# A fixed order of TensorE's work in a two-layer graph attention kernel: fillers between producers and consumers, masks one chunk per beat, two projection chunks per PSUM bank, a second weight queue

## The chip, the core and the metric

The kernel runs on one core of one Trainium2 chip. The metric is the device time of one execution in microseconds (us), lower is better. Each kernel is timed several times in rounds that alternate with the kernel before on the same chip.

The engines: TensorE (PE in the profile; PEld is its weight load), VectorE (DVE), ScalarE (ACT), GpSimd (POOL) and SyncE (SP, which issues transfers). SBUF is the working memory, PSUM the accumulators that TensorE writes.

## The reference, cut to what matters

There are 32 graphs of 512 nodes with 256 features. Each passes through two layers. The first is a transformer layer with masked attention and an MLP, with an outer residual and norm; the second is masked attention with a residual and a norm.

```python
# layer 0
allowed = (adj > 0) | (swapaxes(adj, 1, 2) > 0) | eye          # mask 0
scores  = where(allowed, (q * scale) @ k.T, -inf)              # 8 heads of 32
x1 = layernorm(x + softmax(scores) @ v @ Wo.T + bo) * g1 + be1
h  = layernorm(x1 + relu(x1 @ W1.T + b1) @ W2.T + b2) * g2 + be2
x  = layernorm(x + h)
# layer 1
mask = adjacency == 0                                          # mask 1
x  = layernorm(x + softmax(where(mask, -inf, scores)) @ v @ Wo.T + bo)
```

## The kernel before

The program is a list of 64 slots. A slot is the attention of one graph in one layer, in eight "beats": scores of a chunk of 128 keys for four heads (TensorE), the exponential (ScalarE), the multiply with the 0/1 mask (VectorE), and the product with the values (TensorE). Between the beats, the slot carries other graphs' work. A "forward" slot carries the MLP of the graph whose layer 0 has just ended. An "output" slot carries the output of the graph whose layer 1 has just ended, and the masks of a new graph. The order of emission below is the order on each engine. The comments are mine.

```python
ps_d = pools.enter_context(tc.tile_pool(name="ps_d", bufs=2, space=PSUM))  # two banks for all that is not attention

def masked(self, layer, k):                      # VectorE: the mask multiply, 128 x 2048
    p, m = self.p[k], (self.m0, self.m1)[layer]
    nc.vector.tensor_tensor(p, p, m[:, k % NQ, None, :].to_broadcast([P, HPC, N]), ALU.mult)

def mask0(self, i):                              # TensorE builds adj | adj.T | eye in PSUM ...
    ps = ps_d.tile([P, N], F32, tag="d", name=f"psM_{self.b}_{i}")
    ...
    nc.vector.tensor_scalar(self.m0[:, i, :], ps, 0.0, None, ALU.is_gt)       # ... VectorE empties the bank

def mask1(self, i):
    ps = ps_d.tile([P, N], F32, tag="d", name=f"psN_{self.b}_{i}")
    ...
    nc.vector.tensor_scalar(self.m1[:, i, :], ps, 0.0, None, ALU.not_equal)

def residual(self):                              # GpSimd: two row additions over 128 x 1024
    add_row(self.tile("x1", [NQ, D]), self.x, bov[0])
    add_row(self.x, self.x, be2)

def out1(self, i):                               # one chunk of the projection per bank
    ps = self.projected(1, i)
    y = small.tile([P, D], F32, tag="y", name=f"yl_{self.b}_{i}")
    nc.vector.tensor_tensor(y, ps, self.x2[:, i, :], ALU.add)
    self.y[i] = y, self.statistics(y, 4, i)      # two on VectorE, then add and power on GpSimd

for k in range(BEATS):                           # the output slot, cut
    g.scores(layer, k)
    if k > 0:
        g.masked(layer, k - 1)
    ...
    if k == 2:
        for i in range(NQ):
            last.out1(i)
            if i > 0:
                last.norm4(i - 1)
    elif k == 3:
        last.norm4(NQ - 1); last.store()
        for h in range(2): new.transpose(new.x, h)
        new.residual(); new.mask0(0)
    elif k == 4: new.mask0(1); new.mask0(2)
    elif k == 5: new.mask0(3); new.mask1(0); new.mask1(1)
    elif k == 6: new.mask1(2); new.mask1(3)
    elif k == 7: new.value(0, 0)
    g.product(layer, k - 2)
```

All weights come in on SyncE's queue, ahead of the first graph's x.

## Time and profile before

| | before |
|---|---|
| time, median of the first 3 runs | 3988.58 us (3986.46 to 3989.38) |
| first scores | 45.1 us |
| first slot | 41.3 us |
| forward slot (32 of them) | 72.27 or 73.95 us |
| output slot (30), mean | 50.35 us |
| last slot with the tail | 52.8 us |

A slot is read from the timeline of TensorE as the time from its first scores to the first scores of the next slot.

### The profile page before, as it was taken

The page shows a single profiled execution, that of the slowest core. Times are in us where ns is not written, and L with a number is a line of the kernel's source. Part 1 is how long each engine was busy: PE and PEld are TensorE (multiplying, and loading weights), DVE is VectorE, ACT ScalarE, POOL GpSimd, SP SyncE. Part 2 cuts the span into 40 slices and gives each one's busy share as a digit, 9 for nine tenths or more (in the row PEclk, how much of TensorE's full clock was granted, in tenths as well). Part 3 has the DMA queues.
Part 4 walks back from the last instruction along what each step waited for, and adds up shares of the span by engine and source line. Part 5 has one row for each costly group of instructions (what it writes and reads, how often), then busy time and mean ns, then how long its engine had stood idle before and what let it go on. Part 6 is the DMA issues. An engine that isn't in the chain of part 4 may idle for free.

```text
span 3988.9 us, 51603 instructions
## 1 busy us (share of the span) xinstructions
PE 3643.6 (91%) x21514; PEld 1862.8 (47%) x21514; DVE 2523.0 (63%) x3461; ACT 1606.8 (40%) x1729; POOL 1147.4 (29%) x1545
## 2 busy tenths in 40 slices
PE   7999989899998998989999899998999989999898
PEld 3544535444353443534435354453544535445354
DVE  4566575766757567575665756657566675665765
ACT  3434444334443344344343443434444344343443
POOL 1332322323223132332323323232231322313222
PEclk9999999999999999999999999999999999999999
DMA  2000000000000000000000000000000000000000
GB/s 83 17 22 12 26 11 17 22 22 17 11 17 27 17 22 6 17 27 17 22 6 17 27 17 22 6 17 27 17 22 6 29 15 17 22 6 32 11 1 12
DMA packets 57553, 75.61 MB, mean 19 GB/s; under 512 B 4448, under 2 KB 40416, under 8 KB 57312
## 3 DMA queue, kind: packets, MB, share of 16 engines
q1 hardware_dynamic: 57312, 72.24, 5.5%
q8 instruction: 170, 2.79, 0.3%
q14 instruction: 71, 0.58, 0.0%
HBM read 55.45 MB, written 16.78 MB: 18 GB/s over the span
## 4 chain that ended last, share of the span: by engine, by line
PE 67%; DVE 26%; ACT 3%; POOL 2%; issue 2%; DVEq 0%; ACTq 0%; POOLq 0%
DVE p L277 12%; PE psH L363 12%; PE psF L381 11%; PE psA L290 10%; PE psR L298 9%; PE psQK L255 7%; PE psS L268 7%; PE psV L240 6%; DVE cT L316 3%; PE psO L345 2%; DVE x L406 2%; POOL rs L326 2%; DVE m L209 2%; PE psT L228 2%; ACT xT L231 1%
## 5 line engine op out<-in xcount | busy, mean ns | idle before, releaser
L272 ACT ACTIVATE p<-psS 128x2048 f32<-128x2048 f32 x512 | 961.9, 1879 | 1382.8 <-PE psS L268 1382.8
L277 DVE TENSOR_TENSOR p<-p,m 128x2048 f32<-128x2048 f32 x512 | 1217.4, 2393 | 111.3 <-ACT p L272 111.3
L309 DVE STREAM_TRANSPOSE sT<-psR 128x512 f32<-128x512 f32 x128 | 91.8, 717 | 1074.6 <-PE psR L298 1074.6
L268 PE MATMUL psS<-qT,kT 32*128 32x512 f32 x4096 | 590.5, 646 | 51.8 <-ACT kT L258 51.0
L290 PE MATMUL psA<-p,v 128*32 128x512 f32 x4096 | 555.2, 614 | 1.0 <-DVE p L277 1.0
L298 PE MATMUL psR<-p,ones 128*32 128x512 f32 x4096 | 551.5, 611 | 0.0
L363 PE MATMUL psH<-xT,w_L_gnn_W 128*128 128x256 f32 x2048 | 467.7, 384 | 23.4 <-ACT xT L231 23.4
L326 POOL TENSOR_TENSOR rs<-rs,neg_half 128x1 f32<-128x1 f32 x512 | 462.8, 904 | 42.7
L312 POOL TENSOR_TENSOR total<-total,sT 128x16 f32<-128x16 f32 x128 | 29.0, 226 | 1546.7 <-DVE sT L309 1546.7
L381 PE MATMUL psF<-w_L_gnn_W,hT 128*128 128x256 f32 x2048 | 459.1, 382 | 0.0
L363 PEld LDWEIGHTS psH<-xT,w_L_gnn_W 128*128 128x128 f32 x2048 | 381.2, 190 | 130.0 <-ACT xT L231 55.2
L325 POOL TENSOR_SCALAR rs<-mv 128x1 f32<-128x1 f32 x512 | 213.9, 418 | 789.0 <-DVE mv L324 781.7
L381 PEld LDWEIGHTS psF<-w_L_gnn_W,hT 128*128 128x128 f32 x2048 | 383.8, 190 | 100.7 <-ACT cT L306 26.8
L268 PEld LDWEIGHTS psS<-qT,kT 32*128 32x128 f32 x4096 | 162.8, 186 | 438.0 <-issue 206.7
L371 ACT ACTIVATE hT<-psH,c_L_gnn_b 128x256 f32<-128x256 f32 x512 | 215.0, 471 | 269.0 <-PE psH L363 267.5
L345 PE MATMUL psO<-w_L_gnn_Wo,cT 128*128 128x256 f32 x1024 | 254.2, 395 | 45.2 <-DVE y L339 22.4
L298 PEld LDWEIGHTS psR<-p,ones 128*32 128x32 f32 x4096 | 135.7, 112 | 314.7 <-issue 309.0
L345 PEld LDWEIGHTS psO<-w_L_gnn_Wo,cT 128*128 128x128 f32 x1024 | 179.3, 189 | 142.7 <-ACT kT L258 47.8
L255 PE MATMUL psQK<-xT,w_L_gnn_Wqkv 128*128 128x512 f32 x512 | 236.7, 605 | 0.0
L164 POOL TENSOR_TENSOR x<-x,s_L_gnn_b 128x1024 f32<-128x1024 f32 x32 | 75.4, 2356 | 386.8 <-PE psT L228 386.8
L290 PEld LDWEIGHTS psA<-p,v 128*32 128x32 f32 x4096 | 83.9, 108 | 195.7 <-issue 174.0
L231 ACT COPY xT<-psT 128x512 f32<-128x512 f32 x192 | 109.3, 588 | 122.5 <-PE psT L228 122.5
(68 smaller groups left out, 3363.5 us busy)
## 6 DMA issues: line engine op xcount, KB each, us to landing
adj<-in_adj_dram SPq DMA_DIRECT2D x32, 1024.0 KB, 6.2
x<-in_x_dram SPq DMA_DIRECT2D x32, 512.0 KB, 3.9
out_dram<-x SPq DMA_DIRECT2D x32, 512.0 KB, 2.9
w_L_gnn_W<-in_L_gnn_W_dram SPq DMA_DIRECT2D x2, 1024.0 KB, 9.8
w_L_gnn_Wqkv<-in_L_gnn_Wqkv_dram SPq DMA_DIRECT2D x1, 768.0 KB, 4.8
w_L_gnn_Wo<-in_L_gnn_Wo_dram SPq DMA_DIRECT2D x2, 256.0 KB, 4.4
s_L_gnn_bo<-in_L_gnn_bo_dram SPq DMA_DIRECT2D x2, 128.0 KB, 5.3
s_L_gnn_ln_g<-in_L_gnn_ln_g_dram SPq DMA_DIRECT2D x2, 128.0 KB, 5.6
```

The costliest lines, as they stand in the source:

```text
L240: nc.tensor.matmul(ps[:, j, :], self.xT[:, i, at], proj[layer][0][2][:, i, :], start=(i == 0), stop=(i == ND - 1),)
L255: nc.tensor.matmul(ps, w[:, i, c * P : (c + 1) * P], self.xT[:, i, :], start=(i == 0), stop=(i == ND - 1))
L268: nc.tensor.matmul(s[:, j, :], self.kT[at, hg, kc * P : (kc + 1) * P], self.qT[at, hg, :], start=True, stop=True)
L272: nc.scalar.activation(p, s, AF.Exp, scale=SCALE)
L277: nc.vector.tensor_tensor(p, p, m[:, k % NQ, None, :].to_broadcast([P, HPC, N]), ALU.mult)
L290: nc.tensor.matmul(a[j * HD : (j + 1) * HD, :], self.v[:, kc, h * HD : (h + 1) * HD], p[:, j, :], start=(kc == 0), stop=(kc == NQ - 1),)
L298: nc.tensor.matmul(s[j * HD : (j + 1) * HD, :], ones, p[:, j, :], start=(kc == 0), stop=(kc == NQ - 1))
L326: nc.gpsimd.tensor_tensor(rs, rs, neg_half[:, 0:1], ALU.pow)
L345: nc.tensor.matmul(ps, self.cT[:, k, i * P : (i + 1) * P], wo[layer][:, k, :], start=(k == 0), stop=(k == ND - 1))
L363: nc.tensor.matmul(ps[:, j, :], w1[:, c, at], self.xT[:, c, h * 2 * P : (h + 1) * 2 * P], start=(c == 0), stop=(c == ND - 1),)
L371: nc.scalar.activation(self.hT[h][:, f + j, :], ps[:, j, :], AF.Relu, bias=b1[:, f + j : f + j + 1])
L381: nc.tensor.matmul(ps, self.hT[h][:, f, j * P : (j + 1) * P], w2[:, f, :], start=(f == 0), stop=(f == NF - 1))
```

## The change

The intent is that TensorE never comes to a consumer directly after the producer that it has to wait for. The loop with its conditions becomes two straight lists (`slot_forward`, `slot_output`) with other work between each producer and its consumer. A chunk's two masks are built together, one chunk per beat. Two chunks of the output projection share a PSUM bank. All weights but the first layer's q, k and v move to ScalarE's queue.

```diff
+    def queue(name):
+        return nc.sync if "qkv" in name else nc.scalar
...
+            def project(self, layer, h):
+                ps = ps_d.tile([P, 2, D], F32, tag="d", name=f"psO_{self.b}_{layer}_{h}")
+                for j in range(2):
+                    at = slice((2 * h + j) * P, (2 * h + j + 1) * P)
...
             def out1(self, i):
-                ps = self.projected(1, i)
...
+                self.residual_statistics(self.po[i // 2][:, i % 2, :], self.x2, 4, i)
...
+        def slot_forward(g, layer, last, later):
...
+            g.scores(layer, 7)
+            last.norm2(3)
+            g.masked(layer, 6)
+            last.norm3(2)
+            last.norm3(3)
+            g.masked(layer, 7)
+            g.product(layer, 5)
+            last.transpose(last.x2, 0)
+            g.product(layer, 6)
+            last.value(1, 0)
+            last.transpose(last.x2, 1)
+            g.product(layer, 7)
+            last.query_key(1, 0, 0)
+            last.query_key(1, 1, 0)
+            last.value(1, 1)
...
+        def slot_output(g, layer, last, new, later):
...
+                last.project(1, 0)
+                last.project(1, 1)
+                last.out1(0)
+                last.out1(1)
...
+                new.transpose(new.x, 1)
+                new.residual()
+            g.product(layer, 1)
             for i in range(NQ):
...
+                attend(g, layer, 4 + i)
+                if new:
+                    new.mask0(i)
+                    new.mask1(i)
+                g.product(layer, 2 + i)
```

## The prediction

> **What bounds the kernel now.** I read the page first, then TensorE's waits, then TensorE in order of time over two graphs (1023 to 1272 us), then VectorE and GpSimd there.
>
> ```profile
> PE 3643.6 (91%) x21514; PEld 1862.8 (47%) x21514; DVE 2523.0 (63%) x3461; ACT 1606.8 (40%) x1729; POOL 1147.4 (29%) x1545
> ```
>
> TensorE is busy 91% of a span of 3988.9 us, so its idle time is 345 us. Its waits (who waited for what: us in total, times, longest) say where that is:
>
> ```profile
> PE psN L215 <- DVE m L209: 69.4, 32, 2.3
> PE psS L268 <- ACT kT L258: 51.0, 64, 1.1
> PE psM L203 <- ACT xT L231: 45.0, 31, 1.5
> PE psV L240 <- DVE m L218: 30.2, 29, 1.6
> PE psH L363 <- ACT xT L231: 23.4, 32, 0.7
> PE psV L240 <- ACT xT L231: 23.4, 32, 0.7
> PE psO L345 <- DVE y L339: 22.4, 16, 1.4
> PE psO L345 <- DVE yl L401: 22.4, 16, 1.4
> PE psB L158 <- DMA w_L_gnn_Wo<-in_L_gnn_Wo_dram: 21.6, 2, 14.0
> PE psQK L255 <- ACT xT L231: 21.6, 32, 0.7
> ```
>
> Each but psB is a producer directly ahead of its consumer, or a PSUM buffer not yet emptied; they add to 309 us. The busy time hides one more loss. Columns below: stretch, length, busy us of PE, PEld, DVE, ACT, POOL, TensorE's granted clock, DMA share, GB/s:
>
> ```profile
> 1006.00:1007.00 1.00, 1.00 (x12) 0.13 (x4) 0.11 (x1) 0.59 (x1) 0.00 (x0) 0.70 0.08 16
> 1007.00:1008.00 1.00, 1.00 (x9) 0.21 (x8) 0.09 (x1) 0.00 (x0) 0.00 (x0) 0.50 0.00 0
> 1008.00:1009.00 1.00, 1.00 (x8) 0.31 (x8) 0.93 (x3) 0.00 (x0) 0.23 (x1) 0.50 0.00 0
> ```
>
> After the 2.29 us wait of psN (to 1004.96) the clock is halved from 1006.4 to about 1009.8, which makes 1.7 us of work last 3.4. The same follows the next psN wait at 1053.85. At 32 such waits that is an estimated 54 us more.
>
> The program has 64 slots, each the attention of one graph in one layer. 32 "forward" slots also carry another graph's MLP; 32 "output" slots carry another graph's output and a new graph's masks. Scores to scores, a forward slot takes 72.27 us (1073.28 to 1145.55) or 73.95 (to 1219.50), and output slots average 50.35: between 86.36 and 3936.06 there are 15 times four slots and two forward ones, so (3849.7 - 146.2) / 15 = 246.9 for four. Start (45.1) + first slot (41.3) + 16 x 146.2 + 30 x 50.35 + last slot and tail (52.8) = 3989, the span.
>
> The third view decides how much can be won. VectorE and GpSimd in the output slot (start, length, engine, line):
>
> ```profile
> 1040.18 2.29 DVE L277 TENSOR_TENSOR p<-p,m 128x2048 f32<-128x2048 f32 x1
> 1042.92 2.45 DVE L406 TENSOR_SCALAR x<-yl,mv,rs 128x256 f32<-128x256 f32 x1 [0.45 <-POOL rs L326]
> 1045.29 0.68 DVE L209 TENSOR_SCALAR m<-psM 128x512 bf16<-128x512 f32 x1
> 1045.89 3.90 DVE L277 TENSOR_TENSOR p<-p,m 128x2048 f32<-128x2048 f32 x1
> ```
> ```profile
> 1040.42 2.46 POOL L326 TENSOR_TENSOR rs<-rs,neg_half 128x1 f32<-128x1 f32 x1
> 1042.86 2.36 POOL L164 TENSOR_TENSOR x<-x,bov 128x1024 f32<-128x1024 f32 x1
> 1045.29 2.35 POOL L164 TENSOR_TENSOR x<-x,s_L_gnn_ln_b 128x1024 f32<-128x1024 f32 x1
> ```
>
> A mask multiply (L277) held GpSimd's tiny power up to 2.46 us (0.57 alone); then GpSimd's two row additions held a normalization 2.45 us (0.38 alone) and a multiply 3.90 (2.29 alone). Eviction of masks from PSUM (0.68) ran beside them. VectorE works without a pause worth naming from 1028.28 to 1055: here it, with GpSimd, is the bound, and psN's wait is its symptom.
>
> **What the Trainium skill says.** "SBUF — State Buffer", section "Who interferes with whom": VectorE and GpSimd share a port pair as an exclusive lock, for VectorE operations with two SBUF inputs or in a two-port mode. The lines above agree. "TensorE: Matmul & The Clock Gate", Part 1: the clock halves after an idle window of about 3.4 us and comes back after as long a busy one. The return agrees (3.4 us); but here 2.29 us of idle time was enough, while waits of 1.45 and 1.40 us were followed by full speed. "DMA: Bandwidth & Descriptors", section "Issuing engines are not separate DMA queues": a second queue saves issue time only. Before, the transfer of x was issued at 20.6 us, behind the weights; nothing before has two queues to compare.
>
> **The change, part by part.** Work per operation is unchanged; the order of the built program shows the same matmuls. From start-to-start distances in the timeline: scores 1.07, product 1.86, a q/k pair 3.63, half a value 1.92, projection 3.75, transpose of two chunks 0.53, hidden 14.24, second MLP 14.2, masks of a chunk 0.81.
>
> Forward slot: 8 x 1.07 + 8 x 1.86 + 2 x 3.63 + 3.75 + 4 x 0.53 + 14.24 + 14.2 + 2 x 1.92 = 68.85. Removed are S after kT (0.8), psH, psV and psQK after xT (0.73, 0.73, 0.68) and, in every other slot, psO after y (1.40; two chunks now share a bank, so both banks are free). Added: norm2(3) stands before the multiply of chunk 6. From the end of the MLP (0), VectorE takes 3.0 to the end of norm3(1), 1.64 for norm2(3), 2.2 for the multiply: ready at 6.9 with the handover. TensorE has product 4, scores 7, product 5, transpose: 1.86 + 1.07 + 1.86 + 0.53 = 5.3. A new wait of 1.6. With 0.2 at scores 3 and 0.15 of handovers: 70.8, a gain of 1.5 and 3.15.
>
> Output slot: TensorE work is 42.6 (8 scores, 8 products, two q/k pairs, two half values, projection, two transposes, four masks). But VectorE cannot start on the projection before its bank is full, at 1.07 + 3.63 + 1.07 + 1.88 + 0.07 = 7.7 after the slot's first scores. From there, in program order: two outputs 2.0, multiply 2.2, two norms with the power held behind the multiply 1.1, two outputs 2.0, multiply 2.2, norm, power and the first row addition 3.2, the second addition (2.35), multiply 2.2: chunk 3 is done at 24.9 and mask 0 leaves its bank at 25.5. TensorE is through scores 5 at 21.8 and needs that bank: idle 3.85, and from the 2.29 case a halved clock after it. VectorE goes on: mask 0.6, multiply 2.2, two masks 1.2, wait for product 3 (0.4), the sums' chain 2.46, multiply, two masks, multiply, mask (6.2): 38.6. Only then has the next value its bank. Behind it come value 1.92, product, q, product, k, value (9.3): 49.8. That is 0.5 under before. If the multiply takes the port before the second addition (VectorE's next start and GpSimd's fell on the same 1045.29, so I cannot tell), the chain gives 48.2. So the whole of psN, psM and psV (145 us) with the clock (54) does not come back; it is turned into one larger wait.
>
> Start: x and adj are issued at about 3 us instead of 20.6. But ScalarE must issue 18 transfers before its first copy; SyncE needed some 17 us for such a list. With a table load of 1.3 the first copy moves from 27.5 to perhaps 22, then eight mask evictions (5.6), psB 4.1, q/k and v 7.5: first scores at about 40 instead of 45.1. First slot about 40, last with tail 48.3 (value half and product, 3.8, moved out).
>
> Sum: 40 + 40 + 32 x 70.8 + 30 x 49.8 + 48.3 = 3888; with the kinder port order 3840.
>
> **Rivals.**
> 1. All listed waits vanish and the clock stays up. Then output slots take 43 to 44 and forward ones 69: some 3650. For it: that is the intent. Against it: VectorE's unbroken 27 us in the output slot, untouched by the change.
> 2. As my sum, but the 1.6 us wait in each forward slot trips the clock too: 32 x 1.7 = 54 us more, 3940, within 2% of before. For it: 1.6 lies between 1.45 (harmless) and 2.29 (not).
> 3. The start gets longer because ScalarE is held by transfers: 5 us lost instead of won; it would hardly show.
> 4. Fewer masks per beat relieve VectorE enough that the port's collisions fall elsewhere: 46 to 47 in the output slot, some 3790.
>
> **Range and chances.** Between 3888 and 3840 I lean on neither, and put the time at 3870. Rival 4 sets the lower end, 3790; rival 2 in part of the slots the upper, 3925. 2% faster is 3908.8; the sum has 20 us of margin and its kinder variant 69, hence 0.78 for faster, 0.20 for same, 0.02 for slower, which needs a wait that I have not seen in two places.
>
> **What would show it.** Right: in the waits of TensorE, kT, xT and y are gone; psM after the eviction of psM stands first with 30 times 2 to 4 us; psA after the multiply has 1 to 2 us in forward slots; a low clock still in output slots; slots of about 70.8 and 48 to 50. Wrong: output slots below 46 with a clock of 1.00 (rival 1), or a low clock in forward slots (rival 2), or a first scores later than 45.

## The result

The changed kernel takes 3851.88 us (median of 4 runs, 3850.14 to 3853.78); the kernel before took 3987.52 us in the same rounds. The ratio is 0.9661, 95% interval 0.9644 to 0.9678, so it is 3.4% faster. A ratio here is the mean time of one kernel's fast runs over that of the other's in the same rounds, so it is not quite the ratio of the medians. The prediction was 3870 (3790 to 3925), with 0.78 on faster. All outputs are right.

The first view is the busy time of the engines of the changed kernel (us, share of the span, instructions):

```profile
PE 3608.8 (94%) x21514; PEld 1885.4 (49%) x21514; DVE 2502.6 (65%) x3461; ACT 1603.0 (42%) x1729; POOL 1376.5 (36%) x1545
```

TensorE's idle time went from 345 to 243 us (3851.9 - 3608.8), and its busy time fell by 35 us with the same matmuls. The clock can account for some 9 us of that (22 dips, stretches at half clock, before and 17 after, 1.71 us each; they are counted below); where the rest comes from is not shown. GpSimd's busy time rose by 229 us although it does the same work: the addition in a norm's statistics (`rs<-mv`) went from 214 to 499 us, the power after it from 463 to 327, and the second row addition from 75 to 139. That VectorE blocks it in such a time is shown below for the row addition alone.

The second view is TensorE's waits in the changed kernel (who waited for what: us in total, times, longest):

```profile
PE psM L208 <- DVE m L214: 120.5, 94, 2.0
PE psA L295 <- DVE p L282: 53.6, 37, 1.6
PE psT L233 <- DVE y L341: 16.7, 30, 0.6
PE psM L208 <- ACT xT L236: 12.4, 1, 12.4
PE psT L233 <- DMA x<-in_x_dram: 12.2, 1, 12.2
```

All waits for kT and for xT inside the slots are gone, and so are those of psO for y (0.56 us of psT for y is left in each output slot). In their place, two kinds stand first. In the output slots a mask waits until VectorE has emptied the bank of an earlier mask (psM after m, 94 times). In the forward slots a product waits for its multiply (psA after p). The last two lines happen once each, at the start.

The third view is TensorE in an output slot that began at 992.80 and ended at 1041.13 (start, length, engine, line, operation, idle time before it and who ended it):

```profile
1016.32 0.38 PE L208 MATMUL psM<-edge,ident_b 128*128 128x512 bf16 x1 [1.55 <-DVE m L214]
...
1026.54 0.38 PE L208 MATMUL psM<-edge,ident_b 128*128 128x512 bf16 x1 [1.95 <-DVE m L214]
...
1029.94 1.99 PE L245 MATMUL psV<-w_L_gnn_Wqkv,xT 128*128 128x256 f32 x8 [0.56 <-DVE m L214]
```

With a fourth wait of 0.46 at 1020.68 between the first two, and 0.56 for psT behind y, the slot loses 5.1 us. It takes 48.33 us. The slot ahead of it has the same waits, but there the clock drops after the one of 1.95. Its stretches (us; then busy us of PE, PEld, DVE, ACT and POOL, TensorE's granted clock, DMA share, GB/s):

```profile
976.00:977.00 1.00, 0.00 (x0) 0.00 (x0) 1.00 (x2) 1.00 (x1) 0.00 (x0) 1.00 0.00 0
977.00:978.00 1.00, 0.80 (x10) 0.62 (x9) 1.00 (x3) 0.19 (x1) 0.00 (x0) 1.00 0.00 0
...
980.00:981.00 1.00, 1.00 (x8) 0.00 (x0) 1.00 (x2) 0.00 (x0) 1.00 (x3) 0.50 0.00 0
```

TensorE is idle in the first stretch while VectorE is busy throughout. The pause ends at 977.20, and the clock is at 0.50 from 978.47 to 981.88. That slot took 49.34 us, 1.01 more; the 15 output slots with such a dip take 49.29 on average, the other 15 take 48.32. A dip takes 1.71 us of clock, but part of it only fills the next wait for VectorE: the 0.56 us of psV is missing in the slots that dipped. I counted dips over the whole span from such stretches of 1 us with a clock below 0.95: 21 in the output slots of before, 15 in those of the changed kernel, and one each in the first slot (after only) and the tail (both).

The fourth view is VectorE, then GpSimd, in the slot from 992.80 (start, length, engine, line):

```profile
1011.01 2.46 DVE L411 TENSOR_SCALAR x<-y,mv,rs 128x256 f32<-128x256 f32 x1 [0.45 <-POOL rs L331]
1013.39 2.28 DVE L282 TENSOR_TENSOR p<-p,m 128x2048 f32<-128x2048 f32 x1
1015.59 0.68 DVE L214 TENSOR_SCALAR m<-psM 128x512 bf16<-128x512 f32 x1
...
1016.79 3.24 DVE L282 TENSOR_TENSOR p<-p,m 128x2048 f32<-128x2048 f32 x1
```
```profile
1010.94 2.37 POOL L169 TENSOR_TENSOR x<-x,bov 128x1024 f32<-128x1024 f32 x1
1013.39 4.48 POOL L169 TENSOR_TENSOR x<-x,s_L_gnn_ln_b 128x1024 f32<-128x1024 f32 x1
```

GpSimd's first row addition (L169) holds a norm for 2.46 us; a norm that met nothing took 0.41. At 1013.39 VectorE's multiply and GpSimd's second addition start within 10 ns, and the multiply wins (unrounded, it starts first by 4 to 8 ns in each of the 30 output slots, and wins in each): it takes its normal 2.28 and the addition 4.48 instead of about 2.37. The late addition then holds the next multiply (3.24 instead of 2.28). The bank of mask 0 is emptied only at 1015.59, behind all of this, and TensorE's 1.55 us wait ends there.

In the forward slot, TensorE has one wait:

```profile
1100.03 1.07 PE L295 MATMUL psA<-p,v 128*32 128x512 f32 x8 [1.61 <-DVE p L282]
```

The forward slot takes 70.32 us (1041.13 to 1111.45, and again to 1181.77). The whole of the span in slots: first scores 44.0, first slot 44.1, 32 x 70.32 = 2250.2, last slot with tail 49.3. That leaves 1464.2 for 30 output slots, 48.81 each. Against before, forward slots gave 16 x 146.22 - 2250.2 = 89 us, output slots 30 x (50.35 - 48.81) = 46, the start 1 and the end 3.5; the first slot cost 3. The sum is 137, the difference of the two spans.

### The profile page after: what moved, and what is told of

Same layout as the page of the kernel before. It is cut to its first block, busy times and chain, and to the rows that moved or that the text cites. A ratio compares the mean times of both kernels' runs of the same rounds, so it can differ in the third digit from the quotient of the medians.

```text
span 3851.9 us, 51652 instructions
## 1 busy us (share of the span) xinstructions
PE 3608.8 (94%) x21514; PEld 1885.4 (49%) x21514; DVE 2502.6 (65%) x3461; ACT 1603.0 (42%) x1729; POOL 1376.5 (36%) x1545
## 4 chain that ended last, share of the span: by engine, by line
PE 69%; DVE 23%; POOL 5%; ACT 2%; issue 1%; DMA 0%; ACTq 0%; DVEq 0%; POOLq 0%
PE psQK L260 12%; PE psF L391 12%; PE psH L373 12%; DVE p L282 9%; PE psS L273 8%; PE psA L295 7%; PE psV L245 6%; PE psR L303 6%; PE psO L352 5%; POOL rs L330 4%; DVE st L328 3%; DVE x L411 2%; DVE m L214 2%; ACT p L277 2%; DVE y L341 2%; PE psT L233 1%
## 5 line engine op out<-in xcount | busy, mean ns | idle before, releaser
L282 DVE TENSOR_TENSOR p<-p,m 128x2048 f32<-128x2048 f32 x512 | 1197.4, 2344 | 273.4 <-ACT p L277 273.4
L330 POOL TENSOR_SCALAR rs<-mv 128x1 f32<-128x1 f32 x512 | 499.2, 975 | 1115.0 <-DVE mv L329 1100.3
L373 PE MATMUL psH<-xT,w_L_gnn_W 128*128 128x256 f32 x2048 | 459.1, 382 | 0.0
L331 POOL TENSOR_TENSOR rs<-rs,neg_half 128x1 f32<-128x1 f32 x512 | 327.1, 639 | 42.7
L260 PE MATMUL psQK<-xT,w_L_gnn_Wqkv 128*128 128x512 f32 x512 | 245.0, 611 | 0.0
L252 ACT COPY v<-psV 128x512 f32<-128x512 f32 x128 | 75.0, 586 | 403.3 <-PE psV L245 403.3
L352 PE MATMUL psO<-w_L_gnn_Wo,cT 128*128 128x256 f32 x1024 | 238.4, 386 | 0.5 <-DVE held L768 0.5
L352 PEld LDWEIGHTS psO<-w_L_gnn_Wo,cT 128*128 128x128 f32 x1024 | 189.2, 190 | 72.3 <-ACT kT L263 47.8
L341 DVE TENSOR_TENSOR y<-psO,x 128x256 f32<-128x256 f32 x256 | 104.1, 407 | 152.5 <-PE psO L352 152.5
```

The source lines that it names most:

```text
L260: nc.tensor.matmul(ps, w[:, i, c * P : (c + 1) * P], self.xT[:, i, :], start=(i == 0), stop=(i == ND - 1))
L330: nc.gpsimd.tensor_scalar(rs, mv[:, 1:2], EPS, None, ALU.add)
L331: nc.gpsimd.tensor_tensor(rs, rs, neg_half[:, 0:1], ALU.pow)
L352: nc.tensor.matmul(ps[:, j, :], self.cT[:, k, at], wo[layer][:, k, :], start=(k == 0), stop=(k == ND - 1))
L373: nc.tensor.matmul(ps[:, j, :], w1[:, c, at], self.xT[:, c, h * 2 * P : (h + 1) * 2 * P], start=(c == 0), stop=(c == ND - 1),)
```

## The experiments

My theory had four parts. In the output slot VectorE sets the pace, made late by the two row additions of GpSimd. Pairing the projection delays VectorE further. In the forward slot norm2(3), placed ahead of a multiply, makes the 1.6 us wait. At the start ScalarE's own transfers keep it from its first copy. The rivals were that TensorE's own order bounds the slots whatever VectorE does, and that the parts of the change are each worth what they were meant to be. Eight kernels ran, all edits of the changed kernel. rows_late, single_proj, mult_first and weights_after_x ran beside before at 3989.83 us, the other four beside before at 3987.21; "the changed kernel" is 3851.88 from its own rounds, and a ratio to before is given with each.

### rows_late: GpSimd's row additions at the end of the slot

```diff
                 new.transpose(new.x, 1)
-                new.residual()
...
                 new.query_key(0, 1, 0)
                 new.value(0, 1)
+                new.residual()
```

> The changed kernel with GpSimd's two row additions (x1 and x of the new graph) moved from beat 3 of the output slot to the slot's end. Same work. Theory (VectorE and GpSimd bound the output slot, through the shared port): VectorE's chain loses the 2.0 us in which the norm is held and the 1.0 us in which the fifth multiply is held; output slots go from 48.3 to about 45.5 and most clock dips go, some 30 x 3.2 = 95 us, about 3755 us. Rival (the output slot is held by the masks' two PSUM buffers, whatever VectorE's pace): under 20 us won, psM still waits over 100 us.

Measured: 3747.67 us (ratio 0.9396, 0.9381 to 0.9410), 104 us below the changed kernel, as the theory had it. The output slot takes 45.30 us (966.40 to 1011.70). VectorE at the same place of the slot:

```profile
984.60 0.41 DVE L411 TENSOR_SCALAR x<-y,mv,rs 128x256 f32<-128x256 f32 x1 [0.45 <-POOL rs L331]
984.93 2.28 DVE L282 TENSOR_TENSOR p<-p,m 128x2048 f32<-128x2048 f32 x1
...
988.33 2.28 DVE L282 TENSOR_TENSOR p<-p,m 128x2048 f32<-128x2048 f32 x1
```

The norm is back at 0.41 and the multiply at 2.28: 2.05 + 0.96 = 3.01 us, and the slot without a dip is 48.33 - 45.30 = 3.03 shorter. Dips in the clock fell from 15 to none in the output slots (one is left in the last slot), which is the rest: 30 x (48.81 - 45.30) = 105. The forward slot stayed at 70.31. The additions now hold a 128x512 multiply of the softmax sums instead, 2.39 us at 1010.05, where VectorE has nothing else to do. The theory holds: the loss was the port that VectorE and GpSimd share, and its place in the chain.

### mask1_scalar: take work from VectorE, leave TensorE alone

```diff
-                nc.vector.tensor_scalar(self.m1[:, i, :], ps, 0.0, None, ALU.not_equal)
+                nc.scalar.copy(self.m1[:, i, :], ps)
```

This is a diagnostic: it is right only where adjacency holds zeros and ones, as it does here.

> Diagnostic: the second mask of each chunk leaves PSUM by a copy on ScalarE instead of a comparison on VectorE (valid for adjacency of zeros and ones only, as here). That takes 4 x 0.6 = 2.4 us from VectorE's chain in an output slot and nothing from TensorE. Theory (VectorE bounds the output slot): 1.5 to 2.4 us less per output slot and fewer clock dips, in all 50 to 95 us faster than the changed kernel: 3757 to 3802. Rival (the order of work on TensorE, or a bank that is not free for another reason, bounds it): within 15 us of 3852.

Measured: 3801.21 us (ratio 0.9532, 0.9516 to 0.9548), 51 us faster. The output slot is 47.13 us, 1.2 below the undipped 48.33, and no dip is left outside the tail, since the longest of these waits fell from 1.95 to 1.6. So VectorE is the bound and not the order on TensorE. (The copy also lets another engine free the bank, so this run alone doesn't part VectorE's pace from the bank; rows_late, which leaves the bank's emptying to VectorE, does.) But of the 2.4 us that I took from it only 1.2 came back: the first wait for a mask's bank, which ends before VectorE would have come to its first mask 1, stayed at 1.56. The total lies at the low edge of the range.

### single_proj: one projection chunk per bank again

The first two chunks are projected where pair 0 was, the others after out(0) and out(1) have emptied the banks.

```diff
-                ps = ps_d.tile([P, 2, D], F32, tag="d", name=f"psO_{self.b}_{layer}_{h}")
-                for j in range(2):
-                    at = slice((2 * h + j) * P, (2 * h + j + 1) * P)
+                ps = ps_d.tile([P, D], F32, tag="d", name=f"psO_{self.b}_{layer}_{h}")
+                at = slice(h * P, (h + 1) * P)
...
                 last.out1(0)
                 last.out1(1)
+                last.project(1, 2)
+                last.project(1, 3)
```

> The changed kernel with the projection again one chunk per bank, TensorE's order unchanged. Theory (the order freed the banks, and the pairing itself makes VectorE wait for the second chunk): the first output starts 0.94 us earlier, output slots get up to 0.9 us shorter, no wait of psO over 0.2 us: 0 to 27 us faster than the changed kernel, 3825 to 3852 us. Rival (the pairing is what removed 45 us of psO waits): 20 to 45 us slower, psO after y back in the waits.

Measured: 3815.89 us (ratio 0.9566, 0.9553 to 0.9579), 36 us faster than with pairs, better than the theory's range. The output slot without a dip is 47.45 us. TensorE has no wait of psO; it waits up to 2.2 us for y instead (psT, 30 times, 65 us in total), but the waits for masks fall from 120.5 to 52.2 us, and 5 dips stay of 15. VectorE's first output starts 6.94 us after the slot's first scores and not 7.80, because it no longer waits for the second chunk. These 0.86 us are the 0.88 by which the slot is shorter: 30 x 0.88 = 26 us, as the theory had it, and 10 dips fewer are another 8, which its range had left out. So the pairing is not what removed the psO waits, since single chunks have none either; it only made VectorE, which sets the pace, begin later.

### mult_first: the multiply of chunk 6 ahead of norm2(3)

```diff
-            last.norm2(3)
             g.masked(layer, 6)
+            last.norm2(3)
             last.norm3(2)
```

> The changed kernel with one swap in the forward slot: the multiply of chunk 6 goes ahead of norm2(3) on VectorE. Theory (the 1.61 us wait of product 6 is VectorE's order alone): the wait of psA after the multiply (53.6 us in 37 waits) falls to under 5 us, forward slots go from 70.32 to 68.8 to 69.0, 32 x 1.4 = 45 us, so about 3805 us. Rival (the norms ahead of the transposes then come too late, and the wait only moves to psT or psV): under 10 us won.

Measured: 3832.44 us (ratio 0.9608, 0.9593 to 0.9622), a gain of 19 us and not 45. The wait for chunk 6 vanished, but the forward slot only went from 70.32 to 69.78. TensorE, then VectorE, of this kernel in a forward slot:

```profile
1096.52 1.06 PE L295 MATMUL psA<-p,v 128*32 128x512 f32 x8 [1.03 <-DVE p L282]
```
```profile
1093.86 0.41 DVE L404 TENSOR_SCALAR x<-z,mv,rs 128x256 f32<-128x256 f32 x1 [0.74 <-POOL rs L331]
1094.18 2.28 DVE L282 TENSOR_TENSOR p<-p,m 128x2048 f32<-128x2048 f32 x1
```

The wait moved by one chunk. norm3(3) still stands ahead of the last multiply, it needs GpSimd's power of the statistics that norm2(3) has just made, and VectorE stands still 0.74 us for it. So product 7 waits 1.03. What a reordering wins is bounded by the next thing in the same chain, and I had not followed the chain past the wait that I removed.

### weights_after_x: one queue, the late weights behind x

All weights but the first layer's q, k and v are held back and issued on SyncE's queue after x and adj of the first graph. The sums that need them (value_bias, residual) come after the first values.

```diff
+    held_back = []
+    def issue(name, **kw):
+        if "qkv" in name:
+            nc.sync.dma_start(**kw)
+        else:
+            held_back.append(kw)
...
             graphs[0].load()
+            for kw in held_back:
+                nc.sync.dma_start(**kw)
```

> The changed kernel with one queue: the q/k/v weights, then x and adj of graph 0, then all other weights, and the bias products after the first values instead of ahead of them. Theory (the start is held by ScalarE issuing 18 transfers before its first copy, at 24.5 us, not by the data): first copy at 8 to 14 us, first scores at 32 to 36 us instead of 44.0, 8 to 12 us won, about 3841 us. Rival (the start is held by the 7 MB that have to land): first scores still at 42 to 45, nothing won.

Measured: 3836.94 us (ratio 0.9622, 0.9607 to 0.9636), 15 us faster; the first scores come at 29.9 us instead of 44.0. First the changed kernel's ScalarE, then this one's:

```profile
24.48 1.28 ACT L236 ACT_TABLE_LOAD   x1 [24.48 <-issue]
25.77 1.07 ACT L236 COPY xT<-psT 128x512 f32<-128x512 f32 x2
```
```profile
8.86 0.58 ACT L241 COPY xT<-psT 128x512 f32<-128x512 f32 x1 [6.84 <-PE psT L238]
```

In the changed kernel, ScalarE issues its 18 transfers from 0.73 to 24.45, and only then loads its table and copies; TensorE had had the first transposes ready at 14.1. With the list on the other engine and behind x, the copy is at 8.86. The run changes three things at once (who issues, what comes before x, where the bias sums stand), so it doesn't show what each is worth.

### one_queue: the second queue alone undone

```diff
-        return nc.sync if "qkv" in name else nc.scalar
+        return nc.sync
```

> The changed kernel with the second weight queue alone undone: all weights again on SyncE's queue ahead of x and adj. Theory: the second queue only swapped a late x (before: issued at 20.6 us) for a late first copy of ScalarE (which issued transfers until 24.5 us), so the first scores come within 3 us of the changed kernel's 44.0 us and the time within 5 us of its 3852. Rival: the queue was worth what I predicted for it (5 us at the first scores, or more): 3857 to 3865.

Measured: 3855.55 us (ratio 0.9669, 0.9653 to 0.9685). The total is 3.7 us above the changed kernel, inside what I allowed (the intervals of the two ratios overlap, so the totals don't tell the kernels apart), but the first scores come at 48.97 and not within 3 us of 44.0. On this the rival was right: the second queue is worth 5.0 us at the first scores, in one trace of each. (The traces of the four runs that leave the start alone have them at 42.3 to 44.3.) ScalarE here:

```profile
28.04 0.58 ACT L236 COPY xT<-psT 128x512 f32<-128x512 f32 x1 [26.03 <-PE psT L233]
```

The first copy comes 2.3 us later than in the changed kernel, and GpSimd's coding of adj, which now arrives later too, holds the first mask another 1.4 and 0.6 us. So my reading of the start, a queue that only swaps one delay for another, was wrong. The queue won 5 us there, and the new order of the start gave 4 back: with one queue in both, the first scores went from 45.1 before to 49.0, because the two value-bias sums (psB, 3.2 us) and the second half of the values (some 1.8) now lie between the masks and the first scores.

### masks_grouped: the old grouping of the masks

Masks 1, 2, 3 and 2 at a time in beats 3 to 6, as before, in the changed kernel.

```diff
+                new.mask0(0)
...
-                    new.mask0(i)
-                    new.mask1(i)
+                    if i == 0:
+                        new.mask0(1)
+                        new.mask0(2)
+                    elif i == 1:
+                        new.mask0(3)
+                        new.mask1(0)
+                        new.mask1(1)
+                    elif i == 2:
+                        new.mask1(2)
+                        new.mask1(3)
```

> The changed kernel, but with the eight masks of a new graph in their old grouping (1, 2, 3 and 2 per beat instead of 2, 2, 2, 2). VectorE has the same operations in almost the same order, so my theory that VectorE with GpSimd sets the output slot expects its total wait to stay about the same but to be gathered into fewer and longer pieces (2 to 4 us, after three masks in a row), which halve TensorE's clock in most output slots: 20 to 50 us slower than the changed kernel, 3870 to 3900 us. Rival: how masks are grouped is worth nothing, within 10 us of the changed kernel's 3852.

Measured: 3892.99 us (ratio 0.9762, 0.9746 to 0.9779), 41 us slower, inside the theory's range, but not for the theory's reason. TensorE in an output slot:

```profile
1021.38 0.38 PE L208 MATMUL psM<-edge,ident_b 128*128 128x512 bf16 x1 [2.58 <-DVE m L214]
...
1029.20 0.38 PE L220 MATMUL psN<-ident_b,edge 128*128 128x128 bf16 x4 [2.42 <-DVE m L214]
```

The same work of VectorE makes two pauses of 2.4 to 2.6 us instead of 1.55 and 1.95, and the clock dips 29 times in the 30 output slots. The slots take 49.93 and 50.51 us in the stretch that I looked at. So spreading the masks is worth 41 of the change's 136 us.

By the traces, the clock is the smaller part of it. The one slot without a dip takes 49.93 us, 1.6 more than such a slot of the changed kernel, and its waits add to 6.9 us and not 5.1; so the total wait did not stay the same. (Of the 29 with a dip, 12 take 49.25 to 50.03 and 17 take 50.46 to 51.57.) VectorE, then GpSimd, show why:

```profile
1020.65 0.68 DVE L214 TENSOR_SCALAR m<-psM 128x512 bf16<-128x512 f32 x1
1021.25 3.90 DVE L282 TENSOR_TENSOR p<-p,m 128x2048 f32<-128x2048 f32 x1
```
```profile
1020.66 2.35 POOL L169 TENSOR_TENSOR x<-x,s_L_gnn_ln_b 128x1024 f32<-128x1024 f32 x1
```

The first mask is now emptied ahead of the multiply. The multiply therefore starts 0.59 us after GpSimd's second addition instead of just before it, and this time the addition takes its normal 2.35 while the multiply is held to 3.90 instead of 2.28. It is so in all 30 output slots. These 1.6 us are the difference between the two port orders of the prediction, 49.8 and 48.2: this run measured the order that the changed kernel did not take. Regrouping the masks thus changed the port order too, and no run here changed the grouping alone.

### best: the four gains together

rows_late, mult_first, weights_after_x and single_proj. In the last, out1(2) and out1(3) also move up ahead of the second multiply.

> The four gains together: row additions of the new graph late in the output slot, one projection chunk per bank, the multiply of chunk 6 ahead of norm2(3) and norm3(2) in the forward slot, and on one queue only the q, k and v weights ahead of x. Sum of what they gave alone: 3747.7 (row additions late) - 19 (multiply first) - 15 (weights after x) - up to 27 (30 output slots with 0.9 us less, as the chain starts 1.9 us earlier at the projection): 3685 to 3715. If the single projections overlap with what the late row additions already won, 3710 to 3720.

Measured: 3681.88 us (3680.09 to 3683.04; ratio 0.9234, 0.9218 to 0.9249): 7.7% under before, 170 us under the changed kernel, and 3 us below the expected range. The output slot is 44.12 us, the forward slot 69.83. Its busy times and TensorE's largest waits:

```profile
PE 3576.1 (97%) x21514; PEld 1865.9 (51%) x21514; DVE 2463.5 (67%) x3461; ACT 1601.4 (44%) x1729; POOL 1263.5 (34%) x1545
```
```profile
PE psA L300 <- DVE p L287: 34.2, 35, 1.0
PE psM L213 <- DVE m L219: 21.6, 34, 1.0
PE psV L250 <- DVE m L219: 17.5, 31, 0.6
```

The clock dips nowhere but in the tail. The waits that are left in the slots add to 73 us.

## Why the prediction was right, and where its steps were off

The range held. The predicted 3870 lay between two sums, 3888 and 3840, that differed only by who takes the port on a tie; measured was 3852. That it came so near to 3840 is in part luck: the terms at the end of this section miss by up to 18 us each, with both signs.

**The forward slot** was right: 70.8 predicted, 70.32 measured. The new wait of 1.6 us that I derived from norm2(3) ahead of the multiply is there, with 1.61, and it doesn't trip the clock, so rival 2 fell. The allowance of 0.35 for other waits did not show. My reading of its cause was incomplete, though. mult_first shows that the order of norm2(3) is worth 0.54 us and not 1.6, as the next multiply has the same trouble one chunk later.

**The output slot** was right as a chain of VectorE and GpSimd: 48.33 measured against 48.2 for the kinder port order, and the trace shows the near tie at 1013.39 going that way. The 48.2 is given without its working, but masks_grouped bears out the other order as well: 49.93 in its slot without a dip, against 49.8. rows_late and mask1_scalar show that the chain, and not TensorE's order, sets the slot. Rival 1, with slots of 43 to 44, fell for the changed kernel. But rows_late, which puts two row additions elsewhere, comes to 45.3, and best reaches 44.12: the intent could be met, just not by the order on TensorE alone. Rival 4, which set the lower end of the range, fell too: two collisions are still there (a norm of 2.46, a multiply of 3.24), in a slot of 48.33 and not 46 to 47.

**"Idle 3.85", one wait** was right in its sum and wrong in its shape. (Its own figures, 25.5 less 21.8, give 3.7.) There are three waits for mask banks, 1.55 + 0.46 + 1.95 = 3.96, so the sign "30 times 2 to 4 us" missed: it was 94 times, the longest 2.0. The shape matters for the clock: in these slots no pause of 1.55 us was followed by a dip, and half of those of 1.95 were.

**The term for the clock** was mis-sized. I wrote "At 32 such waits that is an estimated 54 us more" from two cases. Of 30 waits of 2.26 to 2.30 us before, 21 were followed by a dip, so it was 36 us of clock. Not all of that was time, either: in the changed kernel a slot with a dip is 0.97 us longer than one without, and not 1.71, because the slower matmuls use up a wait for VectorE that would have followed. The mean of 48.81 is 48.32 + 0.5 x 0.97, with half of the slots dipped.

**The start and the first slot** were the steps that failed: "first copy moves from 27.5 to perhaps 22" measured 25.77, and "first scores at about 40" measured 44.0. ScalarE's list of 18 transfers took 23.7 us, longer than the 17 us that I had seen for SyncE. Its table load, which had been over at 2 us before, came after the list. The masks ran mostly with waits of 0.35 for each bank, their matmuls took longer than in a slot (the first of a mask 0.58 us and not 0.38), and they took 7.6 us instead of 5.6. Rival 3 named the mechanism, but the second queue still won 5.0 us (one_queue). The first slot took 44.1 and not 40. It has a dip of 1.7 us and a wait of 2.0 for an exponential (psS after p, once), neither in my sum.

Term by term against the sum of 3840: start +4.0, first slot +4.1, forward slots 32 x (70.32 - 70.8) = -15.4, output slots 30 x (48.81 - 48.2) = +18.3, tail +1.0: +12, which gives 3852.

Why the same pause dips the clock in one slot and not in the next can be read from the clock record of the kept traces. In each of the eight traces with several dips, all dips start on one grid of 3.41333 us, to within 3 ns over the whole span. Cut at this grid, from the first scores to the last, the ten traces have 112 stretches followed by a dip, and in each of them TensorE had been idle for at least 1.82 us; of the 10,908 other stretches, seven have more than 1.83 us. So a pause of 1.95 us dips the clock where it falls whole, or nearly so, into one stretch of the grid, and not where the grid divides it. It is the sum that counts, not the single pause: in the last slots of rows_late and mult_first, two pauses of 1.39 and some 0.47 us within one stretch did it too. This is read from the traces; no run moved a pause against the grid on purpose.

What stays open: why three of those seven, with 1.85 to 1.95 us, were not followed by a dip; what the masks' grouping is worth with the port order held; and 26 of the 35 us of TensorE's busy time.

## What to carry to other kernels

Reordering the busiest engine removes its waits only as far as the engines that it waits for have time to spare; before it, follow the second engine's chain in program order and look for operations in it that are far longer than their own kind elsewhere. Here moving two additions of a side engine by half a slot was worth 104 us, nearly as much as the whole rewrite of the order. Where two engines share a port, ask of each pair which operation starts first: here one mask (0.6 us) put ahead of a multiply gave the port to the other engine and made the slot 1.6 us longer. If a pause can't be removed, keep it short and apart from the next: here no pause of up to 1.75 us dropped the clock by itself, half of those of 1.95 did, and two of 1.39 and 0.47 close together did too. And before an engine that computes is given transfers to issue, count how long the list holds it.

## What the Trainium skill lacked or had wrong

- "TensorE: Matmul & The Clock Gate", Part 1, gives an idle window of about 3.4 us before the clock halves. Here some 1.83 us of idle time within a stretch of 3.413 us was enough: of 112 such stretches that were followed by a dip none had less than 1.82. Single pauses of 1.61 us in forward slots never did it, 1.95 did in 15 of 30 output slots, and 2.26 to 2.30 in 21 of 30 before. The page calls the window free-running, and the traces agree: all dips of a trace start on one grid of 3.413 us. The page has no figure for how much idle time within a window is enough.
- "SBUF — State Buffer", "Who interferes with whom", has the lock right (a norm 2.46 us instead of 0.41, a row addition 4.48 instead of 2.37) and says that who issues first takes the port. It doesn't say how small a lead is enough: a multiply that started 4 to 8 ns ahead of the addition kept its 2.28 us in 30 of 30 slots, and one that started 0.59 us behind took 3.90 in 30 of 30 (masks_grouped).
- "DMA: Bandwidth & Descriptors", "Issuing engines are not separate DMA queues", says that issuing on several engines saves only the sequencer's time, usually small. Here it moved the first scores from 49.0 to 44.0 us. The section doesn't say that an engine that issues transfers does not compute meanwhile: ScalarE's first operation waited until 24.48 us, and with the weights behind x on one queue the first scores came at 29.9.
